# Image 0's scan outputs summed into y by TensorE and copied back by ScalarE; the spectral matrices requested one filter ahead

## The chip, the cores and the metric

One core of a Trainium2 chip runs the whole kernel. The metric is device time in microseconds; shorter is better. The kernel before takes 5869.3 us, the median of three runs (5865.73 to 5873.33).

## The reference, cut to what matters

Layer 0 is a selective-scan block (on a group-normalized x), layer 1 attention and a spectral convolution. For each of four images of 48 x 48 positions with 128 channels, layer 0 computes, for four scan directions k and 256 inner channels with 16 states each:

```python
def step(h, inp):
    dt_l, u_l, B_l, C_l = inp
    dA = jnp.exp(dt_l[..., None] * A)
    h = h * dA + (dt_l * u_l)[..., None] * B_l[:, :, None, :]
    y = jnp.einsum('bkdn,bkn->bkd', h, C_l)
    return (h, y)
...
ys = ys + Ds.reshape(1, K, d, 1) * xs
y = ys[:, 0] + ys[:, 2][..., ::-1]
y1 = ys[:, 1] + ys[:, 3][..., ::-1]
y = y + jnp.transpose(y1.reshape(B, d, W, H), (0, 1, 3, 2)).reshape(B, d, L)
```

So the four directions' outputs are added up position by position: k even runs along rows, k odd along columns, k of 2 and 3 backwards. The sum is normalized, gated and projected.

Layer 1's spectral part sums, over 16 filters, a convolution times a 128 x 128 matrix, for four lengths of the sequence with weights of their own. The matrices `M_phi_plus[:, k]` and `M_phi_minus[:, k]` (four of each for a filter) don't depend on the image, so the kernel mixes them once, into matrices called G.

## The kernel before, in words

**The images' stages.** The images go through one after the other. Each has a scan stage (`scans`), then `epilogue` and `attention`; beside an image's scans runs other work that keeps TensorE occupied: for image 0 it is `mixture`, the mixing of the matrices, for the later images the spectral convolution of the image before (`stu`). The order of instructions on each engine is the order in which the program issues them; nothing reorders it. Waits between engines are put in by the framework, from the tiles that instructions share.

**Scans.** An image's scan is cut into 24 chunks: four directions k, six chunks of 384 positions. A chunk has eight units: two halves h of the inner channels, four quarters q of the states. A unit's tile `s` holds 128 partitions (32 channels x 4 states) by four groups g of 384 positions. For each unit:

- `enter` (L481) multiplies dt·u (`rep`) by the rows of B (`bc`): GpSimd for the three units in `POOLED`, VectorE for the others, whose `bc` ScalarE has copied to a PSUM buffer of the ring (`spread`, L473);
- `decay` (L488, L490), on ScalarE, writes exp(dt·A) for one group into a ring buffer;
- `scan` (L497), on VectorE, runs the recurrence of one group, and frees its ring buffer;
- `times_c` (L505, L506), on GpSimd, keeps the last state in `carry` and multiplies by the rows of C;
- `sum_c` (L514), on TensorE, sums over the states by the matrix `csum`, one product for each group, into the PSUM tile `ch.y`. The four quarters accumulate there. There is one such tile (pool `psy`, one buffer);
- after the fourth quarter, `add_y` (L520), on VectorE, adds `ch.y` to the running sum `ya` (`yaccs`), an SBUF tile of 128 x 48 x 48 for each half. `in_order` gives its view: contiguous for even k, strided for odd k. That is 48 additions an image.

For image 0 the ring has five PSUM buffers, shared by decays, spread rows and the small products that prepare later chunks (`prep`, L394 and L408, whose result is stored by DMA as `dtdud` and read back as `rep`). `fill` issues as many decays as buffers are free, so ScalarE runs at most the ring ahead of VectorE.

**Order within a step.** Step s issues: the entries due, the first scan of unit s, `times_c` of unit s-1, the second scan, `add_y` if a half was completed at the end of the step before, the third and fourth scan, and `sum_c` of unit s-2. Between them `more` draws pieces of the other work, in proportion to the columns that TensorE has had.

**DMA.** SP issues the scans' transfers in one queue in program order: `dtdud` (L427), `rep` (L432), `bc` rows (L459, refilled as soon as a row's last user is done), and `mixture`'s transfers.

**`mixture`** goes through 16 filters k. For each it requests the two sets of matrices M (L870, 256 KB each, two buffers each), has ScalarE write eight scaled identities W (L874, L875), and then has TensorE form G in PSUM for q of 0 and 1 by eight products each (L884). A finished G is copied out by ScalarE (L864) and stored (L865) only after the next q's products have been issued, so that of filter k-1's q of 0 comes just before filter k begins.

The epilogue begins with products that read `ya` (L669).

Of the kernel before, what the change touches and what calls it, by code (L numbers as in the profile page):

```python
# [15 lines left out]
P = 128  # L16
B, H, W, C = 4, 48, 48, 128
L = H * W
NJ = L // 256
D, NS, R, K = 256, 16, 8, 4  # L20
NH = D // P
CS = 384
SUB = 384
NT = L // P
G4, DL, C4, Q4 = 4, 32, 4, 4
KF = 16
# [29 lines left out]
def hybrid_kernel(ctx: ExitStack, tc: tile.TileContext, a: dict, out: bass.AP):  # L56
# [3 lines left out]
    nc = tc.nc  # L60
# [7 lines left out]
    ident = wp.tile([P, P], F32, name="ident")  # L68
# [93 lines left out]
    xcs, yaccs, us = {}, {}, {}  # L162

    def prologue(b, pool, mm_tile):
# [8 lines left out]
        xT = pool.tile([P, L], F32, tag="xT", name=f"xT{b}")  # L173
        xpad = pool.tile([P, H + 2, W + 2], F32, tag="xpad", name=f"xpad{b}")
        nc.gpsimd.memset(xpad, 0.0)
        xc = xcs[b] = [keep.tile([P, H, W], F32, tag=f"xc{h}", name=f"xc{b}_{h}") for h in range(NH)]
        rows, parts = SUB // W, SUB // P

# [54 lines left out]
        def proj(h, i, z):  # L233
# [7 lines left out]
            def rest():  # L241
                if z:
# [4 lines left out]
                    return  # L247
                nc.scalar.copy(xpad[:, 1 + i * rows:1 + (i + 1) * rows, 1:W + 1],
                               now["ps"][:, :SUB].rearrange("p (r w) -> p r w", w=W))
# [63 lines left out]
    def in_order(t, k, lo, n):  # L313

        if k % 2 == 0:
            return t[:, lo // W:(lo + n) // W, :]
        return t.rearrange("p h w -> p w h")[:, lo // H:(lo + n) // H, :]
# [143 lines left out]
    class Unit:  # L461
# [46 lines left out]
        def sum_c(self, ps):  # L508

            ch = self.ch  # L510
            if self.q == 0:
                ch.y = ps.tile([P, 512], F32, tag="y", name=f"y{self.name}")
            for g in range(G4):
                nc.tensor.matmul(ch.y[g * DL:(g + 1) * DL, :CS], csum, self.s[:, g], start=(self.q == 0),  # L514
                                 stop=(self.q == Q4 - 1))

        def add_y(self):
            ch = self.ch
            v = in_order(yaccs[ch.b][self.h], ch.k, ch.lo, CS)
            nc.vector.tensor_tensor(v, v, ch.y[:, :CS].rearrange("p (r w) -> p r w", w=v.shape[2]), ALU.add)  # L520

    NCH = L // CS
# [332 lines left out]
    def mixture(pool, ps):  # L855

        late = []
        banks = [0]  # L860

        def keep_(p, k, q):
            G = pool.two.tile([P, NF, C], F32, tag="Gm", name=f"Gm{k}_{q}")
            nc.scalar.copy(G, p)  # L864
            nc.sync.dma_start(gd[k, :, q], G)  # L865

        for k in range(KF):
            M = [pool.two.tile([P, NF, C], F32, tag=f"M{j}", name=f"M{j}_{k}") for j in range(2)]
            for t, src in zip(M, ("M_phi_plus", "M_phi_minus")):
                nc.sync.dma_start(t, a[src][:, k].rearrange("i d e -> d i e"))  # L870

            W = pool.two.tile([P, 2, NF, P], F32, tag="W", name=f"W{k}")
            for i in range(NF):
                nc.scalar.activation(W[:, 0, i], ident, AF.Copy, scale=ws[:, k, i:i + 1])  # L874
                nc.scalar.activation(W[:, 1, i], nident, AF.Copy, scale=ws[:, k, i:i + 1])  # L875
            yield 0
            for q in range(2):
                p = ps.psc.tile([P, NF, C], F32, tag=("x", "y")[banks[0] % 2], name=f"G{k}_{q}")
                banks[0] += 1
                for i in range(NF):  # L880

                    n = NF - i
                    for t in range(2):
                        nc.tensor.matmul(p[:, :n], W[:, q if t else 0, i],  # L884
                                         M[t][:, i].unsqueeze(1).to_broadcast([P, n, C]),
                                         start=(t == 0 and i == 0), stop=(t == 1 and i == NF - 1))
                        yield n * C
                if late:
                    keep_(*late.pop())
                late.append((p, k, q))  # L890
        keep_(*late.pop())
# [309 lines left out]
    for b in range(B):  # L1201
# [3 lines left out]
        if b == 0:  # L1205
            mixed = Stage(tc, "m", "right", two=(2, SB))
            scans(b, *first, front, sp, ps, ring, mixture(mixed, ps), MIX_COLS)
            mixed.close()
        else:
            scans(b, *first, front, sp, ps, ring, stu_alone(b - 1, ps, 1), STU_COLS)  # L1210
# [99 lines left out]
```

## Time and profile before

| what | us |
|---|---|
| median of 3 runs | 5869.3 |
| the profiled execution | 5877.4 |
| its span, first to last instruction | 5875.7 |
| image 0's scan stage in it | 118 to 1099 |
| VectorE busy in that stage | 924.7 of 981.0 |
| GpSimd busy in that stage | 878.8 |
| ScalarE busy in that stage | 651.7 |
| TensorE busy in that stage | 527.0 |

The page gives one execution. A group's line names line of code, engine, operation, output and inputs, shape, and for each group the idle time of the engine just before it and what ended that. Times in a time line are from the start of the span. Idle time on an engine that isn't the one that sets the end costs nothing. The costliest groups of the whole run are the scans' own:

```profile
L497 DVE TENSOR_TENSOR_SCAN s<-ring,s 128x385 f32<-128x385 f32 x3072 | 2706.4, 939 | 120.7 <-ACT ring L490 118.9
L506 POOL TENSOR_TENSOR s<-s,bc 128x1536 f32<-128x1536 f32 x768 | 2439.1, 3178 | 129.5 <-DVE s L497 74.9
L490 ACT ACTIVATE ring<-rep,A 128x384 f32<-128x384 f32 x3072 | 1759.6, 584 | 816.8 <-DVE s L481 461.6
L514 PE MATMUL y<-s,csum 128*32 128x384 f32 x6144 | 717.0, 541 | 183.8 <-POOL s L506 106.8
```

### The profile page before, as it was taken

How to read it: one execution, taken by the hardware profiler on the slowest of the kernel's cores; microseconds unless marked ns; L12 is line 12 of the kernel's file. 1: busy time of each engine (PE TensorE's matmuls, PEld its weight loads, DVE VectorE, ACT ScalarE, POOL GpSimd, SP SyncE). 2: the span in 40 equal slices, each digit the busy share in tenths (PEclk: the TensorE clock that was granted, in tenths of full speed). 3: DMA queues.
4: the chain of work that ended last, by engine and by line, in shares of the span. 5: the costliest groups of instructions: out<-in, count | busy, mean ns of one | idle time of the engine just before them, and what ended most of it. 6: DMA issues, size and time to landing. Idle time of an engine off the chain costs nothing. (4 is left out here: it accounts for less than half of the span.)

```text
span 5875.7 us, 73876 instructions
## 1 busy us (share of the span) xinstructions
PE 4903.8 (83%) x23826; PEld 3137.6 (53%) x23826; DVE 4281.4 (73%) x4931; ACT 3310.1 (56%) x6909; POOL 3621.0 (62%) x1823
## 2 busy tenths in 40 slices
PE   3555554598999998797999998779999998889999
PEld 1111111344566666545566666536566666468889
DVE  6999999746999999457999998548999997200000
ACT  2666666346777776246777765247777764332111
POOL 1999898504888998306898998107899986000000
PEclk6677767798999999898999999889999999999999
DMA  3444444216777778126887787027877785045546
GB/s 107 155 163 154 163 157 160 71 31 188 230 250 240 259 254 273 56 68 196 241 254 245 249 265 251 29 82 219 249 248 253 250 263 192 14 114 157 158 147 208
DMA packets 750563, 1066.85 MB, mean 182 GB/s; under 512 B 158528, under 2 KB 561088, under 8 KB 750144
## 3 DMA queue, kind: packets, MB, share of 16 engines
q1 hardware_dynamic: 744352, 1058.83, 57.3%
q10 hardware_dynamic: 5824, 3.30, 0.3%
q8 instruction: 190, 3.11, 0.2%
q14 instruction: 197, 1.61, 0.1%
HBM read 943.80 MB, written 117.98 MB: 181 GB/s over the span
## 5 line engine op out<-in xcount | busy, mean ns | idle before, releaser
L497 DVE TENSOR_TENSOR_SCAN s<-ring,s 128x385 f32<-128x385 f32 x3072 | 2706.4, 939 | 120.7 <-ACT ring L490 118.9
L506 POOL TENSOR_TENSOR s<-s,bc 128x1536 f32<-128x1536 f32 x768 | 2439.1, 3178 | 129.5 <-DVE s L497 74.9
L490 ACT ACTIVATE ring<-rep,A 128x384 f32<-128x384 f32 x3072 | 1759.6, 584 | 816.8 <-DVE s L481 461.6
L481 POOL TENSOR_TENSOR s<-rep,bc 128x1536 f32<-128x1536 f32 x288 | 994.0, 3451 | 137.5 <-DMA bc<-xdd 132.1
L481 DVE TENSOR_TENSOR s<-rep,ring 128x1536 f32<-128x1536 f32 x480 | 831.5, 1733 | 72.9 <-ACT ring L473 28.2
L1041 PE MATMUL cx<-tt,us 128*128 128x254 f32 (+7 forms) x3840 | 819.5, 356 | 74.1 <-ACT U L1065 48.5
L514 PE MATMUL y<-s,csum 128*32 128x384 f32 x6144 | 717.0, 541 | 183.8 <-POOL s L506 106.8
L1041 PE MATMUL cx<-tt,u 128*128 128x254 f32 (+7 forms) x3840 | 809.7, 354 | 66.0 <-ACT cy L1057 65.8
L1041 PE MATMUL cy<-tt,u 128*128 128x252 f32 (+5 forms) x3840 | 796.2, 351 | 28.2 <-DMA tt<-fd 28.2
L1041 PEld LDWEIGHTS cx<-tt,u 128*128 128x128 f32 x3840 | 642.5, 191 | 310.8 <-issue 114.3
L1041 PEld LDWEIGHTS cx<-tt,us 128*128 128x128 f32 x3840 | 646.8, 193 | 273.8 <-issue 89.7
L1041 PEld LDWEIGHTS cy<-tt,u 128*128 128x128 f32 x3840 | 647.3, 192 | 175.7 <-issue 113.5
L1104 PE MATMUL pr<-U,G 128*128 128x288 f32 (+6 forms) x2048 | 590.4, 420 | 17.5 <-DMA G<-gd 17.5
L1131 DVE TENSOR_TENSOR res<-res,ot 126x512 f32<-126x512 f32 (+1 forms) x20 | 13.4, 671 | 687.1 <-PE ot L1125 687.1
L884 PE MATMUL G<-M,W 128*128 128x256 f32 (+3 forms) x512 | 247.3, 601 | 246.2 <-DMA M<-in_M_phi_plus 141.1
L1104 PEld LDWEIGHTS pr<-U,G 128*128 128x128 f32 x2048 | 340.8, 191 | 171.9 <-issue 96.5
L514 PEld LDWEIGHTS y<-s,csum 128*32 128x32 f32 x6144 | 127.0, 112 | 545.6 <-issue 287.6
L770 ACT ACTIVATE e<-s,shift 128x512 f32<-128x512 f32 (+1 forms) x360 | 230.9, 643 | 331.1 <-PE s L768 330.5
L156 POOL TENSOR_TENSOR ln_vu<-ln_vu,mhalf 128x4 f32<-128x4 f32 (+1 forms) x20 | 21.8, 1091 | 626.1 <-DVE ln_vu L155 626.1
L768 PE MATMUL s<-xnT 128*128 128x512 f32 (+1 forms) x720 | 357.5, 582 | 45.8 <-ACT xnT L730 23.3
L761 PE MATMUL o<-e,xn 128*128 128x512 f32 (+1 forms) x720 | 342.4, 559 | 4.5 <-ACT e L770 4.5
L1064 ACT COPY U<-cx 128x252 f32<-128x252 f32 (+1 forms) x320 | 111.4, 348 | 399.4 <-PE cx L1041 396.9
(167 smaller groups left out, 4030.7 us busy)
## 6 DMA issues: line engine op xcount, KB each, us to landing
rep<-dtdud SPq DMA_DIRECT2D x768, 384.0 KB
bc<-xdd SPq DMA_DIRECT2D x3072, 48.0 KB
tt<-fd SPq DMA_DIRECT2D x192, 577.0 KB
tt<-fd SPq DMA_DIRECT2D x192, 505.0 KB
dtdud<-re SPq DMA_DIRECT2D x192, 384.0 KB
tt<-fd SPq DMA_DIRECT2D x192, 379.0 KB
G<-gd SPq DMA_DIRECT2D x192, 256.0 KB
tt<-fd SPq DMA_DIRECT2D x64, 506.0 KB
```

The lines of the kernel that those rows point to most:

```text
L481: eng.tensor_tensor(s, self.ch.rep[self.h][:, :, 1], bt.unsqueeze(1).to_broadcast([P, G4, CS]), ALU.mult)
L490: nc.scalar.activation(ring.body(self.dA[g]), ch.rep[self.h][:, g, 0], AF.Exp, scale=A[:, ch.k, self.h * G4 + g, self.q:self.q + 1])
L497: nc.vector.tensor_tensor_scan(s, ring.decays(i, ch.rev), s, 0.0, ALU.mult, ALU.add)
L506: nc.gpsimd.tensor_tensor(self.s, self.s, ch.bc[Q4 + self.q].unsqueeze(1).to_broadcast([P, G4, CS]), ALU.mult)
L514: nc.tensor.matmul(ch.y[g * DL:(g + 1) * DL, :CS], csum, self.s[:, g], start=(self.q == 0), stop=(self.q == Q4 - 1))
L761: nc.tensor.matmul(po[J][:, :w], xn[:, i], e[:, :w], start=(i == 0), stop=(i == NT - 1))
L768: nc.tensor.matmul(p[:, :w], xnT[:, i * P:(i + 1) * P], xnT[:, 512 * J:512 * J + w], start=True, stop=True)
L770: nc.scalar.activation(e[:, :w], p[:, :w], AF.Exp, bias=shift)
L884: nc.tensor.matmul(p[:, :n], W[:, q if t else 0, i], M[t][:, i].unsqueeze(1).to_broadcast([P, n, C]), start=(t == 0 and i == 0), stop=(t = ...
L1041: nc.tensor.matmul(p4[:, 1:3, v - (hi - at):] if g else p4[:, 0:4:3, v - (hi - at):], x, t[:, :, hi - 1 - at + J * P:end if end >= 0 else ...
L1064: nc.scalar.copy(U[n][:, 2:8:5], p[:, :4 * (w + 1)].rearrange("p (e m) -> p e m", e=4)[:, 0:4:3, 1:])
L1104: nc.tensor.matmul(o if q else o.rearrange("p f r m -> p r f m"), G, U[n][:, 4 * q:4 * q + 4, v0:v1].rearrange("p (a b) m -> p a b m", a=2 ...
```

## The change

Two edits. For image 0 (`ch.b == 0`) the running sum is no longer added by VectorE: after the last quarter's products TensorE also multiplies the old values of `ya` by the identity into the same PSUM tile, and ScalarE copies the finished sum from PSUM over the old values. The later images keep VectorE's addition. And `mixture` requests filter 0's and 1's matrices when it starts, and then filter k+1's where it requested filter k's; the buffers stay at two of each.

```diff
@@ -513,10 +513,16 @@
             for g in range(G4):
                 nc.tensor.matmul(ch.y[g * DL:(g + 1) * DL, :CS], csum, self.s[:, g], start=(self.q == 0),
                                  stop=(self.q == Q4 - 1))
+            if ch.b == 0 and self.q == Q4 - 1:
+                nc.tensor.matmul(ch.y[:, :CS], ident, in_order(yaccs[ch.b][self.h], ch.k, ch.lo, CS), start=False,
+                                 stop=True, skip_group_check=True)
 
         def add_y(self):
             ch = self.ch
             v = in_order(yaccs[ch.b][self.h], ch.k, ch.lo, CS)
+            if ch.b == 0:
+                nc.scalar.copy(v, ch.y[:, :CS].rearrange("p (r w) -> p r w", w=v.shape[2]))
+                return
             nc.vector.tensor_tensor(v, v, ch.y[:, :CS].rearrange("p (r w) -> p r w", w=v.shape[2]), ALU.add)
 
     NCH = L // CS
@@ -864,11 +870,15 @@
             nc.scalar.copy(G, p)
             nc.sync.dma_start(gd[k, :, q], G)
 
-        for k in range(KF):
+        def fetched(k):
             M = [pool.two.tile([P, NF, C], F32, tag=f"M{j}", name=f"M{j}_{k}") for j in range(2)]
             for t, src in zip(M, ("M_phi_plus", "M_phi_minus")):
                 nc.sync.dma_start(t, a[src][:, k].rearrange("i d e -> d i e"))
-
+            return M
+
+        ahead = fetched(0)
+        for k in range(KF):
+            M, ahead = ahead, fetched(k + 1) if k + 1 < KF else None
             W = pool.two.tile([P, 2, NF, P], F32, tag="W", name=f"W{k}")
             for i in range(NF):
                 nc.scalar.activation(W[:, 0, i], ident, AF.Copy, scale=ws[:, k, i:i + 1])
```

## The prediction

> **What bounds the kernel now.** I read the slices first: image 0's scans lie in slices 1 to 7, where VectorE is fullest and GpSimd next.
>
> ```profile
> PE   3555554598999998797999998779999998889999
> DVE  6999999746999999457999998548999997200000
> ACT  2666666346777776246777765247777764332111
> POOL 1999898504888998306898998107899986000000
> ```
>
> The table by stretches gives the stage's figures: columns are length, then busy us (instructions) of PE, weight loads, VectorE, ScalarE, GpSimd; then clock, DMA share, GB/s.
>
> ```profile
> 118.00:1099.00 981.00, 526.98 (x2178) 168.64 (x2179) 924.70 (x980) 651.73 (x1361) 878.83 (x427) 0.71 0.48 157
> ```
>
> VectorE is busy 94% of the 981 us, GpSimd 90%, ScalarE 66%, TensorE 54%: VectorE leads, with GpSimd close behind. Nothing outside this stage is edited; the chain of waits covers only the last part of the run and says nothing here.
>
> Next the additions themselves, in the steady part (160 to 1075 us), then who waits for whom there (total, times, longest):
>
> ```profile
> L520 DVE TENSOR_TENSOR ya<-ya,y x46: 522/555/857, 162.0 to 1069.0; 128x384 f32<-128x384 f32 x46
> ```
>
> ```profile
> DVE ya L520 <- PE y L514: 25.4, 12, 4.9
> DVE s L481 <- POOL s L506: 5.0, 3, 1.7
> ...
> PE G L884 <- DMA M<-in_M_phi_plus: 107.3, 12, 13.3
> PE G L884 <- ACT Gm L864: 74.2, 15, 10.5
> PE y L514 <- POOL s L506: 71.7, 40, 5.1
> ...
> POOL carry L505 <- DVE s L497: 56.2, 32, 3.1
> POOL s L506 <- DVE s L497: 13.8, 9, 3.3
> ```
>
> VectorE's largest wait is the one before its addition, for TensorE's y; and TensorE is late there because it stood before a filter's first product, waiting for M. The time line shows the longest case (start, length, engine, line, operation, idle before):
>
> ```profile
> 741.88 0.58 ACT L864 COPY Gm<-G 128x512 f32<-128x512 f32 x1
> 742.36 0.40 ACT L874 ACTIVATE W<-ident,ws 128x128 f32<-128x128 f32 x1
> 742.91 0.39 SPq L870 DMA_DIRECT2D M<-in_M_phi_plus  x1
> ...
> 746.02 2.05 PE L884 MATMUL G<-M,W 128*128 128x512 f32 x2 [13.33 <-DMA M<-in_M_phi_plus]
> ...
> 748.00 1.51 PE L514 MATMUL y<-s,csum 128*32 128x384 f32 x8
> ...
> 749.65 0.55 DVE L520 TENSOR_TENSOR ya<-ya,y 128x384 f32<-128x384 f32 x1 [4.93 <-PE y L514]
> ```
>
> M lands 3.1 us after its request. So of TensorE's 13.3 us only that much is the transfer; the rest is ScalarE reaching the copy of Gm and the first W, which stand in ScalarE's order.
>
> [...] TensorE's durations below are the trace's.
>
> **The change part by part** (steady part, and the whole stage where said).
>
> *Additions removed from VectorE.* 48 in image 0. By starts of the next instruction they hold the engine 0.44 us for even k (161.99 to 162.43) and 0.72 for odd k, where ya is walked across rows (482.56 to 483.28): 24 x 0.44 + 24 x 0.72 = 27.8 us.
>
> *VectorE's wait for y removed.* VectorE no longer meets y at all: 25.4 us. (In the whole stage it is 30.8 us in 13 times; the last, 5.3, is the drain at the end and stays with whoever reads y.) Together 53.2 us.
>
> *Copies added to ScalarE.* 48 of 128 x 384: 0.47 (L411) for even k; for odd k, a strided write that no row shows, between 0.47 and VectorE's strided 0.86; I take 0.6. About 26 us. ScalarE stands 260 us of the steady part waiting before its decays for VectorE to free ring buffers, so as busy time this fits. What matters is the wait: each copy waits for y, and the decays (L490) queued behind it wait too, and VectorE's scans for those. Cover: the ring has five buffers; ScalarE reaches the copy as soon as the step's first scan is done, with three to five scans' decays already made (one buffer may hold spread rows, one a projection). At 0.86 us a scan that is 2.6 to 4.3 us; less the copy and the next decay (0.5 + 0.6) leaves 1.5 to 3.2 us of waiting for y that costs nothing. VectorE found y ready one scan (0.86 us) after that point in 35 of 48 cases; those cost nothing. Of the other 13, the four long ones (3.5, 4.1, 4.9, 3.6) shrink with the next item. I put 2 us in all for what pokes through: not below nothing, since a queued copy can't make a decay earlier, and at most the third rival's 72.
>
> *Products added to TensorE.* 48 of 128 x 384 by the identity. The nearest row is L408 (mean 754 ns), L394 runs 486 to 1009 with odd k's stride in it: 0.75 each, 36 us with weight loads at most 45. TensorE waits over 250 us in the steady part, so its time is hidden; y comes 0.75 us later each time, inside the cover above.
>
> *M a filter ahead.* Same bytes, same number of requests. TensorE now waits for Gm and the first W only: in the case shown product G could start at 742.8 instead of 746.0. That is 3.2 us for 15 filters, 48 us off TensorE's waits, none of it on the path by itself; it takes about 3 us off each long wait for y. The filter's first M still comes when the generator starts, so TensorE's first wait, and VectorE's 10.3 us at 145 us, stay. On SP's queue, the request for k+1 now waits until TensorE has finished k-1; behind it stand bc rows. TensorE's 12 waits for M are at least 6.9 us long against 3.1 of transfer, so it had finished at least 3.7 us before the request: no wait. For the three other filters I take nothing; at 3 us each it would be 9. The second filter's two requests at the start (1.0 us of SP, 0.5 MB) stand before chunk 1's dtdud and rep, which are used some 25 us later: nothing, at most 4.
>
> *At the stage's end* the chain GpSimd, y, addition (0.84) becomes y, product 0.75, copy 0.5: +0.4.
>
> *Where the stall goes.* GpSimd is next. Its waits for VectorE are 56.2 + 13.8, some 70 us in 915: its floor for the steady part is 845, VectorE's new sum 915 - 53 = 862. So GpSimd would be 98% busy. With so little slack each holds the other at times. VectorE waited for GpSimd's products 5.0 us[...]. I take 7 us more in all, bounds 0 (more load on GpSimd can't shorten a wait for it) and 30 (the first rival).
>
> Sum: -53.2 + 2 + 0.4 + 7 = -44 us. The profiled execution took 5877.4 us (span 5875.7), so it would take 5833.4; the median of the runs shown, 5869.3, lies 8.1 below the profiled one, which gives 5825.
>
> **Rivals.**
>
> *GpSimd takes the bound early.* For: 90% against 94% busy, and a chunk's 11 large GpSimd operations come in bunches (eight products at 3.43 us start to start with the carry, three entries at 3.4: 37.6 of 40.0 us a chunk). Against: VectorE waited for it only 5 us. If GpSimd keeps two thirds of its 70 us of waits, the stage loses only 23 us: 5846.
>
> *The request ahead buys nothing and the copies' waits eat the rest.* TensorE already waits for ScalarE's Gm copy, and M's landing may have hidden a slower W. The copies then lose about what the additions held: within 0.2% (12 us, about what a measurement of this kernel can tell from no change), 5869.
>
> *The copy starves the scans: slower.* One mechanism: ScalarE stands before each copy until y and its identity product are done, decays queue behind, the ring runs dry, VectorE idles. It decides at 53/48 = 1.1 us of starvation per copy; at 1.5 us the stage is 72 - 53 = 19 us longer: 5888. For: it holds if y on average comes more than about 3 us after the step's first scan. Against: y was there within 0.9 us in 35 of 48.
>
> **How the numbers follow.** Forecast (5812 to 5832; the low end if nothing pokes through and a few more of VectorE's 12 us of other waits go): 0.60. GpSimd early (5832 to 5857): 0.22. No change (5857 to 5881): 0.08. Starvation (above 5881): 0.10. The first two hold 0.82, so the range is 5812 to 5857; faster 0.82, same 0.08, slower 0.10.
>
> **What would show it.** Right: image 0's scans end near 1054 instead of 1098 us; VectorE has no wait for y in that stage; GpSimd is above 94% busy there; TensorE's waits for M are gone but those for Gm or W stay; ScalarE waits for y a few tens of us while VectorE's waits for the ring stay under 10. Wrong: VectorE waiting for the ring by tens of us (starvation), its entries or products waiting for GpSimd by tens (the first rival), or SP held before M with bc rows late. Images 1 to 3 must keep their times; if they move, the sum has missed something.

## The result, and the profile after

The kernel takes 5849.8 us after the change (median of 7 runs, 5847.9 to 5857.8) against 5873.1 before on the same chips (median of 7). The ratio is 0.9964, with a 95% interval of 0.9954 to 0.9973: about 21 us faster, clear of no change, and half of the 44 us that were forecast. The profiled execution took 5857.8 us (before: 5877.4). Image 0's scan stage ends at about 1082 instead of 1099 us. Its last scan starts 21 us earlier than before, those of images 1 to 3 start 26, 17 and 19 us earlier: the gain is made in image 0, and the later images move by a few us either way.

The slices of the profile after:

```profile
PE   3566555697999998788999998779999998889999
DVE  6999999657999998548999997548999997200000
ACT  2777777346777776247777775247777764332111
POOL 1999999505889998207889997108898986000000
```

VectorE is as full as it was in slices 1 to 6, though 48 additions were taken from it. The rows of the copies and of the identity products, from the steady part (160 to 1050 us; count, then shortest, median and longest ns):

```profile
L517 PE MATMUL y<-ya,ident x90: 486/822/1009, 178.5 to 1045.1; 128*128 128x384 f32 x90
L524 ACT COPY ya<-y x46: 468/479/825, 160.7 to 1049.1; 128x384 f32<-128x384 f32 x46
```

A product is two records here (90 for 45), so it takes twice what I read off L408's mean: 72 us in all instead of 36. The copies are 0.47 us for even k and 0.81 for odd k. Who waits for whom, in the same stretch:

```profile
DVE s L481 <- issue: 11.7, 8, 1.8
DVE s L481 <- ACT ring L473: 8.8, 5, 2.2
DVE s L497 <- ACT ring L490: 6.6, 13, 2.7
DVE s L481 <- POOL s L506: 1.2, 1, 1.2
...
PE G L894 <- ACT W L884: 80.3, 14, 10.1
PE G L894 <- ACT Gm L870: 71.8, 15, 9.9
...
POOL carry L505 <- DVE s L497: 43.9, 23, 2.5
POOL s L506 <- DVE s L497: 9.1, 5, 3.8
```

TensorE waits for M no more, only for W and Gm. VectorE's wait for y is gone. GpSimd, which was to be next, still waits 53 us for VectorE (70 before), in 28 places, about one a chunk. If VectorE has so much less to do and waits so little, why does GpSimd still wait for it?

The answer is in an operation that I had priced at 5 us in all, an estimate of mine within the 7 us of *Where the stall goes*: L438, dt times u, two a chunk, with both inputs in SBUF. Its groups, before and after (instructions, then busy us, mean ns, and idle time ahead of it):

```profile
L438 DVE TENSOR_TENSOR re<-re,xc 128x384 f32<-128x384 f32 x44 | 41.5, 984 | 0.0
```

```profile
L438 DVE TENSOR_TENSOR re<-re,xc 128x384 f32<-128x384 f32 x44 | 58.0, 1359 | 0.0
```

The same instruction got 38% longer. Its shortest is 0.53 us for even k and 0.8 for odd k, 0.68 on average; the rest is waiting, booked as busy time. The time line of the same chunk shows what it waits for, before and after:

```profile
245.08 3.17 POOL L506 TENSOR_TENSOR s<-s,bc 128x1536 f32<-128x1536 f32 x1
246.40 2.73 DVE L438 TENSOR_TENSOR re<-re,xc 128x384 f32<-128x384 f32 x2
249.06 0.94 DVE L497 TENSOR_TENSOR_SCAN s<-ring,s 128x385 f32<-128x385 f32 x1
250.07 0.19 POOL L505 COPY carry<-s 128x4 f32<-128x4 f32 x1 [1.81 <-DVE s L497]
```

```profile
242.99 3.18 POOL L506 TENSOR_TENSOR s<-s,bc 128x1536 f32<-128x1536 f32 x1
243.35 3.69 DVE L438 TENSOR_TENSOR re<-re,xc 128x384 f32<-128x384 f32 x2
246.97 0.95 DVE L497 TENSOR_TENSOR_SCAN s<-ring,s 128x385 f32<-128x385 f32 x1
247.98 0.19 POOL L505 COPY carry<-s 128x4 f32<-128x4 f32 x1 [1.81 <-DVE s L497]
```

In both, VectorE comes to L438 while GpSimd is in the middle of a product (L506), and gets through only when that has ended (248.25 and 246.17). Behind L438 stands the unit's last scan, and for that GpSimd then waits 1.81 us. After the change VectorE arrives earlier within GpSimd's product, stands longer, and leaves at the same point of GpSimd's round. So it goes throughout the trace after: 19 of the 44 products L438 start inside a GpSimd product, and each of them ends 0.41 to 0.71 us after that one has; the other 25 take 0.53 to 0.85 us. What makes L438 stand no run shows. My theory after the result, called the lock cycle below (the lock, or the lock wait, is a name for L438's standing until GpSimd's product has ended), was: in image 0 a chunk takes GpSimd's own 37.6 us plus this 1.8 to 2.4 us, some 39.5 us, whatever VectorE saves; the gain comes from the few chunks that had a long wait for M. The 37.6 was the prediction's sum of single operations and is a little high: over 18 chunks (2 to 19) of the trace after, GpSimd's work comes to 37.1 us a chunk and its waits to 2.5, together 39.6; before, it was 37.1 and 3.1. The times from one chunk's first scan to the next chunk's, worked out from the traces' scans, agree:

```
chunk     8     9    10    11    12    13    14    15    16    17    18    19    20    21
before  42.2  39.7  39.4  42.2  40.5  40.3  39.1  42.9  39.8  39.5  40.5  39.7  42.9  39.7
after   39.7  39.7  39.2  38.8  39.1  40.9  39.2  39.6  39.8  38.6  39.8  39.8  39.8  39.7
```

The chunks of 42 to 43 us, those with a wait for M, shrank to 39 or 40; most others stayed. The rest of the 21 us was gained in the first two chunks and the last ones. The rival theories: VectorE still leads, and ScalarE's new work eats the gain; or GpSimd's load alone is the bound.

### The profile page after: what moved, and what is told of

The parts are those of the page before. It is cut to its first block, busy times and chain, and to the rows that moved or that the text cites. A ratio compares the mean times of both kernels' runs of the same rounds, so it can differ in the third digit from the quotient of the medians.

```text
span 5856.1 us, 74080 instructions
## 1 busy us (share of the span) xinstructions
PE 4937.2 (84%) x23922; PEld 3149.3 (54%) x23922; DVE 4267.9 (73%) x4883; ACT 3333.3 (57%) x6957; POOL 3622.6 (62%) x1823
## 5 line engine op out<-in xcount | busy, mean ns | idle before, releaser
L506 POOL TENSOR_TENSOR s<-s,bc 128x1536 f32<-128x1536 f32 x768 | 2440.0, 3179 | 128.5 <-DVE s L497 73.3
L481 POOL TENSOR_TENSOR s<-rep,bc 128x1536 f32<-128x1536 f32 x288 | 994.4, 3453 | 131.2 <-DMA bc<-xdd 124.2
L481 DVE TENSOR_TENSOR s<-rep,ring 128x1536 f32<-128x1536 f32 x480 | 831.4, 1733 | 86.6 <-ACT ring L473 36.5
L894 PE MATMUL G<-M,W 128*128 128x256 f32 (+3 forms) x512 | 233.2, 571 | 189.1 <-ACT W L884 80.3
```

The lines of the kernel that those rows point to most:

```text
L481: eng.tensor_tensor(s, self.ch.rep[self.h][:, :, 1], bt.unsqueeze(1).to_broadcast([P, G4, CS]), ALU.mult)
L506: nc.gpsimd.tensor_tensor(self.s, self.s, ch.bc[Q4 + self.q].unsqueeze(1).to_broadcast([P, G4, CS]), ALU.mult)
L894: nc.tensor.matmul(p[:, :n], W[:, q if t else 0, i], M[t][:, i].unsqueeze(1).to_broadcast([P, n, C]), start=(t == 0 and i == 0), stop=(t = ...
```

## The experiments

All changes below are for image 0 alone; ratios are to the kernel before, run on the same chip in the same session.

**Each half alone.** Run e1: the sum by TensorE and the copy by ScalarE, without the request ahead:

```diff
-        ahead = fetched(0)
         for k in range(KF):
-            M, ahead = ahead, fetched(k + 1) if k + 1 < KF else None
+            M = fetched(k)
```

> The sum by TensorE and the copy by ScalarE as in the changed kernel, the matrices requested as before. Theory 1 (lock cycle): in image 0 a chunk takes GpSimd's 37.6 us plus about 1.9 in which GpSimd waits for a scan that stands behind the product dt*u (L438) on VectorE[...]; VectorE's freed time only lengthens that wait, and the gain comes from the long waits for y alone. The long waits are then cut by ScalarE's cover (1.5 to 3 us each in 8 to 12 cases): 8 to 18 us below before, ratio 0.997 to 0.9986. Theory 2 (VectorE is the bound, and the gain is eaten by ScalarE's new work): the additions' 28 us are most of the gain, so nearly all of the changed kernel's 23 us, ratio about 0.996.

Measured: 5868.5 against 5870.5 us, ratio 0.9997 (0.9989 to 1.0006): nothing. That is less than even theory 1 had expected, and the time line says why. It is the case that the prediction showed, TensorE late for M:

```profile
742.85 2.05 PE L893 MATMUL G<-M,W 128*128 128x512 f32 x2 [13.37 <-DMA M<-in_M_phi_plus]
744.83 1.51 PE L514 MATMUL y<-s,csum 128*32 128x384 f32 x8
746.27 1.46 PE L517 MATMUL y<-ya,ident 128*128 128x384 f32 x2
747.76 0.48 ACT L524 COPY ya<-y 128x384 f32<-128x384 f32 x1 [4.61 <-PE y L517]
748.14 0.49 ACT L473 COPY ring<-bc 128x384 f32<-128x384 f32 x1
748.72 1.75 DVE L481 TENSOR_TENSOR s<-rep,ring 128x1536 f32<-128x1536 f32 x1 [5.50 <-ACT ring L473]
```

The wait for y has moved from VectorE's addition (4.93 us) to ScalarE's copy (4.61), and from there straight back: behind the copy stands the row to be spread (L473), which VectorE's next entry (L481) needs. VectorE waits 5.50 us. My cover had counted decays only. So this run doesn't tell what the additions' own time is worth.

Run e2: the request ahead, with the additions left on VectorE (the diff's other half):

> The matrices requested a filter ahead, the additions left on VectorE. Theory 1: each long wait for y is shorter by the 3.2 us of the transfer, 10 to 18 us below before, ratio 0.997 to 0.9983; the chunks without a long wait stay at 39.4 to 39.7 us although VectorE still adds. Theory 2: the additions still cost their 28 us, so less than 10 us below before, and 15 us or more above the changed kernel.

Measured: 5853.1 against 5870.5, ratio 0.9970 (0.9959 to 0.9981), 17 us faster. Its intervals overlap with the changed kernel's 0.9964. VectorE's wait for y, still there, fell from 25.4 us to this:

```profile
DVE ya L520 <- PE y L514: 7.4, 6, 1.7
DVE s L481 <- POOL s L506: 5.0, 3, 1.7
```

So the request ahead, by itself, makes most of the gain, and the move of the additions adds little or nothing to it.

**VectorE's time.** Run e4: the changed kernel with other work put back on VectorE in the additions' place:

```diff
...
             if ch.b == 0:
                 nc.scalar.copy(v, ch.y[:, :CS].rearrange("p (r w) -> p r w", w=v.shape[2]))
+                nc.vector.tensor_reduce(extra, xcs[ch.b][self.h].rearrange("p h w -> p (h w)")[:, :CS], AX.X, ALU.max)
                 return
```

> The changed kernel with a reduction of 128 x 384 (one SBUF input, some 0.5 us, result unused) on VectorE in the place of each addition of image 0: 48 of them, some 25 us of VectorE time. Theory 1: VectorE stands 1.8 us a chunk in the lock wait beyond what the product needs, so this costs nothing: within 5 us of the changed kernel. Theory 2: VectorE is the bound, so 20 to 25 us above the changed kernel.

Measured: 5849.3 against 5870.5 us, ratio 0.9969 (0.9958 to 0.9979), the changed kernel's 0.9964 within its interval. Some 25 us of work on VectorE cost nothing that can be measured. L438's total fell from 62.0 to 51.3 us over the stage, and VectorE's other waits in the steady part from 28.9 to 22.1: the work took the place of some 18 us of waiting, and the rest is within what the intervals can tell. VectorE's work doesn't set the time of the changed kernel.

**L438's wait.** Run e3: L438 given one input in PSUM, so that it no longer has two in SBUF; the additions before have one in PSUM, and none took over 0.86 us beside GpSimd's operations:

```diff
...
+            if ring:
+                nc.scalar.copy(ring.body(i), re[:, 0, 0])
             yield 0
...
-                dt, dx = [re[:, h, i].rearrange("p (r w) -> p r w", w=x.shape[2]) for i in range(2)]
+                dt, dx = [t.rearrange("p (r w) -> p r w", w=x.shape[2])
+                          for t in (ring.body(i) if ring else re[:, h, 0], re[:, h, 1])]
                 nc.vector.tensor_tensor(dx, dt, x, ALU.mult)
```

> The changed kernel, and in image 0 (from the third chunk's preparation on, where the ring exists) the product dt*u (L438) reads dt from a ring buffer in PSUM, to which ScalarE copies it, so that it has one SBUF input; the second half's product comes two calls later. Theory 1: without two SBUF inputs it doesn't wait for GpSimd, a chunk takes 37.8 to 38.3 us instead of 39.5, 25 to 35 us below the changed kernel, 5815 to 5826 us; L438 takes 0.55 to 0.85 us each time. Theory 2: no gain over the changed kernel, up to 20 us slower, since ScalarE has two more copies a chunk and the ring one buffer less.

Measured: 5840.7 against 5870.5, ratio 0.9951 (0.9939 to 0.9964), some 8 us below the changed kernel by the ratios, with intervals that overlap; the 25 to 35 us that were expected didn't come. The wait inside L438 did go (it is L444 there, 30.1 us for 44 products instead of 58.0), but VectorE now waited 14 us for ScalarE's copy of dt. Run e9, with the second product one call (of the generator `prep`, which prepares a chunk piece by piece) later:

> The kernel whose product dt*u reads dt from PSUM, with the second half's product one call later (VectorE stood 14 us there waiting for ScalarE's copy). Lock cycle, with ScalarE's order as the next limit: those waits go, 5 to 12 us below the kernel with the product in PSUM; if the ring buffer held one call longer starves the scans instead, the same or slower.

Measured: 5840.5 against 5873.7, ratio 0.9946 (0.9932 to 0.9959); no change that can be told instead of 5 to 12 us, and the wait for ScalarE stayed at 12.9 us. So it wasn't the call that set it.

Run e5: L438 on GpSimd instead:

> The changed kernel with image 0's product dt*u (L438) on GpSimd instead of VectorE; GpSimd keeps its three entries a chunk. Lock cycle: GpSimd's 1.9 us gap a chunk goes, but the two products cost it about 0.9 us each, so 37.6 + 1.8 = 39.4 us a chunk as before: within 8 us of the changed kernel. If VectorE's occupancy were the bound, the 62 us that L438 takes on it would go: 20 us or more below the changed kernel.

Measured: 5845.8 against 5876.9, ratio 0.9949 (0.9935 to 0.9962), some 9 us below the changed kernel by the ratios; in its trace GpSimd has not one gap over 0.4 us between 170 and 1030 us. With the products added (1.1 us each) it is full, at 39.0 us a chunk. So GpSimd's load is the second wall, close behind the first: 37.1 us without them.

Run e6: with one of GpSimd's three entries given to VectorE as well; e7: the same without moving L438; e8: e6 with the additions back on VectorE. The entry's diff:

```diff
-            self.pool = (h, q) in POOLED
+            self.pool = (h, q) in (POOLED if ch.b else ((0, 3), (1, 3)))
```

> As the run before, and in image 0 only two of a chunk's eight entries on GpSimd: one (3.4 us) goes to VectorE (1.65 us). GpSimd 37.6 + 1.8 - 3.4 = 36.0 us a chunk, VectorE 27.6 (scans) + 6 x 1.65 = 37.5[...]. Lock cycle: a chunk takes 37.7 to 38.4 us instead of 39.5, 22 to 38 us below the changed kernel, 5812 to 5828. If ScalarE's order set the pace (copies, spread rows), no gain, since it gets one more row to spread a chunk.

> The changed kernel with only two entries on GpSimd in image 0, the product L438 left on VectorE. Lock cycle: GpSimd has slack (34.2 us a chunk), but VectorE now needs 37.5 + 0.9 to 1.6[...]: 39.5 to 40.5 us, 0 to 20 us above the changed kernel. If GpSimd's load alone were the bound: 20 us below it.

> The run with the product on GpSimd and two entries there, but with the additions back on VectorE (matrices still a filter ahead). With the lock out of the way VectorE leads (37.5 us a chunk), so the additions' 1.2 us a chunk should now cost what was expected of them at first: 15 to 28 us above the run without them. If they cost nothing here either (under 6 us), VectorE doesn't lead there.

Measured: 5848.5 (0.9955, 0.9942 to 0.9969), 5863.5 (0.9980, 0.9971 to 0.9989) and 5859.5 (0.9968, 0.9955 to 0.9980), all against 5876.9. The first missed its 22 to 38 us: VectorE waited 35 us for ScalarE (rows to spread, ring), of which the page puts 16.5 to "issue"; those waits end 0.1 us after a copy of L473. The second is slower than the changed kernel by some 9 us (the intervals just meet), as the lock cycle had it, but not for its reason: L438 didn't wait there at all.

```profile
L438 DVE TENSOR_TENSOR re<-re,xc 128x384 f32<-128x384 f32 x44 | 28.3, 683 | 0.0
```

None of the 44 starts inside a GpSimd operation. GpSimd, with less to do, waits for VectorE's scans instead (118 us in the steady part, 53 in the changed kernel), since the entry that was moved costs VectorE 1.73 us a chunk, some 40 us in the stage: VectorE is busy 731 of 760 us (210 to 970 us), with none of L438's waiting in it. So this run moved load from GpSimd to VectorE, and doesn't tell what relieving GpSimd alone is worth. The third shows additions costing 11 us by the medians (8 by the ratios) once L438 is off VectorE, less than the 15 to 28 expected and within overlapping intervals.

**The row behind the copy.** Run e10: the sum on TensorE and ScalarE alone again, with the copy issued one scan later, so that the row stands ahead of it:

```diff
-            if pending:
+            if pending and pending[-1].ch.b:
                 pending.pop().add_y()
             prepare(s)
             more((s + 0.5) / len(units))
             spread(s + 2)
             if real:
                 scan(s, 2)
+            if pending:
+                pending.pop().add_y()
...
```

> The sum on TensorE and ScalarE alone (matrices requested as before), with image 0's copy issued after the step's third scan instead of after its second, so that the row to spread (L473), which VectorE's next entry needs, stands ahead of the copy on ScalarE and not behind it. If the row behind the copy is what passed the wait for y on to VectorE: the entries' wait for L473 falls from 17 us to under 6, and the time is 8 to 16 us below the run with the copy in its first place, 5852 to 5862. If TensorE's lateness reaches VectorE through the decays in any case: within 5 us of that run.

Measured: 5859.8 against 5873.7, ratio 0.9977 (0.9968 to 0.9986): 14 us faster where the copy in its first place gained nothing. The entries' wait for L473 fell from 17.4 to 1.2 us, and with those that the page puts to other causes, but that end within 0.12 us after a copy of L473, from 33 to 12. The scans' wait for decays rather rose (15.5 to 20.5), so it was the row that counted.

Run e13: in the changed kernel, the same move alone, to tell what L438's wait with GpSimd's load does to the chunks from what the row behind the copy does:

> The changed kernel with image 0's copy issued after the step's third scan, nothing else. [...]within 5 us of the changed kernel, the time given by ScalarE going into a longer L438. If the row behind the copy is what ate the gain: 8 to 14 us below the changed kernel, ratio to before 0.994 to 0.995.

Measured: 5847.6 against 5868.2, ratio 0.9963 (0.9952 to 0.9975), the same as the changed kernel. VectorE's other waits fell by 10 us (28.8 to 18.3 between 160 and 1030 us), and more than half of that went into L438 again; its group there:

```profile
L438 DVE TENSOR_TENSOR re<-re,xc 128x384 f32<-128x384 f32 x44 | 64.4, 1502 | 0.0
```

It grew from 1359 to 1502 ns, in total from 58.0 to 64.4 us. So in the changed kernel L438's wait, with GpSimd's own load, holds the chunks, and the row behind the copy doesn't.

**Both obstacles away.** Run e11: e9 with the late copy; e12: e3 with the additions back on VectorE:

> The changed kernel with the product from PSUM (second half's one call later) and the copy issued after the third scan. Lock cycle, and the row behind the copy: both gains add up, 15 to 28 us below the changed kernel, 0.991 to 0.9945 of before. If ScalarE's load is the limit once the lock is gone: no better than the product from PSUM alone, 0.995.

> The product from PSUM with the additions back on VectorE (matrices a filter ahead): the fourth corner of additions on VectorE or not, with the lock wait or without. Lock cycle: with the lock wait the additions cost 3 us; without it they cost 8 to 25 us over the run with the product from PSUM. If they cost under 5 us here too, VectorE's time is not what moving them frees, lock or no lock.

Measured: 5828.0 (0.9928, 0.9915 to 0.9942) and 5838.5 (0.9945, 0.9932 to 0.9957), both against 5873.7. The first went as forecast. It is the fastest kernel of the study, 21 us below the changed kernel by the ratios, with intervals apart, and 42 us below before (46 by the medians); that this is near the 44 us of the prediction is chance, for it takes two more edits. Its product's group, and its waits:

```profile
L444 DVE TENSOR_TENSOR re<-ring,xc 128x384 f32<-128x384 f32 x44 | 30.2, 686 | 14.8 <-ACT ring L427 13.7 <-DMA bc<-xdd 1.1
```

```profile
DVE s L512 <- ACT ring L505: 9.1, 13, 2.8
DVE s L496 <- issue: 6.3, 5, 1.7
...
POOL carry L520 <- DVE s L512: 22.8, 23, 2.7
POOL s L521 <- DVE s L512: 7.7, 6, 2.8
```

L444's longest is 0.84 us, and GpSimd's waits for VectorE are 30 us instead of the changed kernel's 53; a chunk takes 38.5 us instead of 39.6, with the same operations on GpSimd. The second kernel missed its 8 to 25 us: with the product from PSUM but the copy in its first place (0.9951, 0.9946) moving the additions gains nothing over leaving them on VectorE (0.9945). Against e11 it is 10 us slower, and all five runs of one lie below all five of the other, in the same session: only with both obstacles away is the move worth something, and then some 10 us.

Run e14: VectorE's time once more, in the fastest version:

> The version with the product from PSUM and the copy after the third scan, with 48 reductions of 128 x 384 (some 0.5 us each, result unused) on VectorE in the place of the additions. They cost nothing in the changed kernel. If VectorE leads here, 10 to 26 us above the version without them, 0.9945 to 0.997 of before; if GpSimd or ScalarE leads here as well, under 5 us above it, 0.9925 to 0.9937.

Measured: 5831.7 against 5868.2, ratio 0.9941 (0.9929 to 0.9953). It lies 8 us above the version without the reductions by the ratios, between the two expectations, and the intervals meet: whether VectorE leads there stays open. In the two profiles image 0's last scan starts at 1059.5 with the reductions and at 1048.7 us without, which speaks for it, though the profile without them is of the fastest of its five runs.

## Why the prediction was right in direction and wrong in size

**The direction and the place were right**: faster, all in image 0's scans, images 1 to 3 within some 10 us; VectorE's wait for y gone; TensorE's waits for M gone and those for Gm and W left; SP never held before M. The result lies within the range that was given, but in the part of it that was the first rival's.

**The step that failed is the first of "What bounds the kernel now": VectorE leads, so what is taken from it comes off the stage.** VectorE was 94% busy, but part of that was waiting: L438's 41.5 us in the steady part are 28.3 where none of them starts inside a GpSimd operation (e7), 58.0 after the change. And the chunk's round ran through GpSimd: 25 us of work put back on VectorE cost nothing (e4). I had priced L438's waiting as an average (the 5 us) without asking what stands behind L438 on VectorE and who waits for that. In the traces each L438 that starts inside a GpSimd product stands until that has ended: 14 of 44 before, 19 of 44 after. With one input moved to PSUM (e11), L438's mean falls from 1359 to 686 ns and its longest from 3566 to 840. The chunk's round before the change was GpSimd's 37.1 us, with a gap in it for L438 and the scan behind it, and in some chunks the long wait for y.

**The sum, term by term.** *Additions, -27.8 us*: nothing that can be told in the changed kernel (e4: their time put back costs nothing; changed kernel against e2: 3 us, within the intervals). *Wait for y, -25.4*: with M ahead alone 18 of them left VectorE's waits and 17 us the time. I had given M's request "none of it on the path by itself"; it is the larger part of the gain. *Cover of ScalarE's copy, +2*: the cover was missing its nearest customer. I counted three to five decays behind the copy; the row to spread stands right behind it and is needed after two more scans. Measured by e10 against e1: about 12 us, in a kernel where M still comes late. *Identity products*: 72 us and 22 of weight loads instead of at most 45 together, one record taken for a whole product; hidden all the same, TensorE still waits over 250 us. *GpSimd, +7*: L438's wait grew by 16.5 us in the steady part where I had put 5, and VectorE's other waits grew from 11.8 to 28.9, of which 27 end with ScalarE's rows and decays. So the account of the 53 us taken from VectorE closes roughly: 16.5 into L438, 17 into these other waits, some 20 into the time.

**The first rival** gave 5846 and the result was 5850: its sign and size were right, and its place, GpSimd, in part. But it named the bunching of GpSimd's operations, and e11 rules that out as the whole cause: with the same operations on GpSimd a chunk got 1.1 us shorter. What GpSimd's load alone is worth no run tells (e7 gave the load to VectorE). **The starving copy** is a real mechanism too (e1), at about 0.25 us a copy instead of the 1.1 from which it turns the sign.

**What stays open**: what VectorE's and ScalarE's shares are in the 1.4 us by which the fastest version's 38.5 us a chunk exceed GpSimd's work (e14's interval). And what makes L438 wait for the end of GpSimd's operation. In the steady part before, 14 of the 44 products L438 start inside a GpSimd operation, and none of these ends before it does; of the additions, with one input in PSUM, 44 of 45 start inside one, 34 of these end before it, and none takes over 0.86 us. With one of its inputs in PSUM (e11), 38 of the 44 products start inside a GpSimd operation and 34 end before it. These versions also draw the two products apart and let them wait for ScalarE, so it isn't the input alone that changed, and no run shows what holds the product.

## What to carry to other kernels

Before counting an engine's busy time as its work, compare an operation's mean with its shortest for the same access pattern (here 0.98 us against 0.52 and 0.79): the difference may be a wait, and time taken from that engine may only lengthen it. Where a stage's rounds take the same time with or without some work on an engine, look for a cycle between engines; follow it, here GpSimd's product, L438, scan, GpSimd, and break it before moving work. And when a wait is handed to another engine, look at the very next instruction behind it in that engine's queue and at who needs it first.

## What the runs showed of the hardware that was not expected

- A VectorE product of two SBUF operands, 128 x 384, took 0.53 us (0.79 where it walks across rows) at its shortest and up to 3.57 us where it started inside a GpSimd product: all 19 that did so in the trace after ended 0.41 to 0.71 us after that product. Its waiting counts as busy. With one operand in PSUM (e11) it took 0.84 us at most.
- ScalarE's copy of 128 x 384 from PSUM takes 0.47 us into contiguous rows and 0.81 us into ones walked across (stride of 192 bytes), in the same step as VectorE's addition (0.55 and 0.82).
- An fp32 product of 128 x 384 by the identity (L517) appears as two records, together some 1.1 to 1.9 us on TensorE in the trace after.
- The dt times u product of 128 x 384 takes 1.0 us (even k) or 1.2 (odd k) on GpSimd (e5, mean 1107 ns), where 0.9 had been scaled down from its larger products.
